# Attention with its scores in one bank and a three-bank tile, divisors formed two units later, and the next image's norm placed beside the projections

## The chip, the cores and the metric

The kernel runs on one core of one Trainium2 chip, as one launch. The metric is device time in microseconds of one execution. A core has five engines with their own instruction queues: TensorE (PE, matmuls; its weight loads are shown as PEld), VectorE (DVE), ScalarE (ACT), GpSimd (POOL) and SyncE (SP, which here only issues DMAs). They are ordered among each other by semaphores alone. PE writes into PSUM, which is eight banks of 2 KB per partition (512 float32 each); ACT and DVE read it.

## The reference

Four images of 256 channels and 48 x 48 pixels go through two layers, each added to its input. All arithmetic is float32.

```python
x = x + L0(_gn(x))      # _gn: group norm, 32 groups
x = x + L1(_gn(x))

def L0(Vx, ...):        # 3x3 conv, batch norm, relu, then attention with 8 heads of 32 channels
    x = relu(bn(conv(Vx, conv_w) + conv_b))          # N = 48*48 = 2304 pixels
    q, k, v = split(einsum('oc,bchw->bohw', qkv_w, x) + qkv_b)
    attn = softmax(einsum('bhdn,bhdm->bhnm', q, k) * 32 ** -0.5, axis=-1)
    out = einsum('bhem,bhnm->bhen', v, attn)
    return einsum('oc,bchw->bohw', proj_w, out) + proj_b

def L1(x, ...):         # guidance conv, 5 branches of 9 shifted taps weighted by a softmax
    guidance = conv3x3(x, W_cat)                     # 45 channels
    outs = [x] + [dyn_branch(x, softmax(guidance[:, 9*i:9*i+9]), d)
                  for i, d in enumerate((1, 6, 12, 24, 36))]
    y = conv1x1(concat(outs), W_scale)
    return batch_norm_over_all_images(y) * gamma + beta
```

## The kernel before, in words

Everything of an image stays in SBUF: channels on the 128 partitions in two halves (`NH = 2`), pixels along the free axis. Two kinds of stages alternate. In an **attention stage** (function `attention`) image b is attended to. In a **mixed stage** (`dynamic_filters`) the second layer of image b is computed by DVE and POOL, and the convolution and the q, k, v of image b + 1 are woven into it for PE. The program is issued in one written order (`tc.manual_schedule()`): each engine executes its instructions in the order of the Python code, and a tile pool makes an instruction wait where a buffer is still in use.

**An attention stage** is cut into nine units. Units 0 to 7 are 512 queries of one half of the heads (four heads, j = 0 to 3, on four groups of 32 partitions); unit 8 holds the last 256 queries of both halves. A unit loops over the keys in 18 steps of 128 (`m`). A step (u, m) is:

- `scores(u, m)`: four matmuls k^T q, one for each head, side by side on 32 rows of the array each, 128 x 512 results. They go to PSUM tiles `se`. Before, these are two tiles of two banks (a pair of heads in each), from a pool of three such tiles (`ps_s`, bufs=3, six banks). Two ACT instructions then form p = exp(scale * s), 128 x 1024 each (L961). `p` has four buffers.
- `weigh(u, m - 1, p)`: one step behind, four matmuls v p, side by side on 32 columns each, add into the PSUM tile `num` (one bank, one buffer, L982). DVE adds p to the running sum `acc` (L999, 128 x 2048) from which the softmax's divisors come. In the steps `LENT = (2, 5, 8, 11, 14)` DVE adds only heads 0 and 1 (128 x 1024); heads 2 and 3 of that p are summed into the SBUF tile `extra` by a DMA that POOL issues (L1001 writes, L1003 accumulates). At the unit's last step DVE adds `extra` to `acc` (L991), and ACT copies `num` to SBUF (L1008) so that the next unit can begin in its one bank.
- `close(u - 1)`, at m = 2 of the next unit: four matmuls of ones with `acc` give the divisors (`den`, a bank of its own, L1014); DVE transposes, inverts and transposes back (L1023 to L1026), and multiplies into the result `ao` (L1031).
- `project(chunk)`, at m = 6 of units 2, 4, 6 (two chunks) and 8: eight matmuls of 384 columns on finished `ao` (L1063), a bias and residual addition and statistics on DVE (L1072, L605), and a DMA to HBM. The sixth chunk is done at the start of the mixed stage.
- The group norm of image b + 1 (b < 3): `finish` (three short stages of statistics with two tiny matmuls in the `den` bank) and twelve ACT instructions that normalize the next image in place (L1715, 128 x 384 each). They are the list `spare`, of which one is taken at each step from m = 3 of unit 2.

The eight PSUM banks of the stage are thus three pairs for scores and projections, `num`, and `den`.

**Around the stage.** At the end of a mixed stage `done(5)` copies the last chunk's y from PSUM to an SBUF tile `y` with ACT (L1301), DVE takes statistics, and SP sends it to HBM (L1309). `load_pad(b)` and `load_pad(b + 1)` then load x into the two padded images (L1692), behind it on SP. The tiles `p` of the attention stage lie in the memory that the mixed stage's tiles leave.

Of the kernel before, what the change touches and what calls it, by code (L numbers as in the profile page):

```python
# [8 lines left out]
F32 = mybir.dt.float32  # L9
F32R = mybir.dt.float32r  # L10
AF = mybir.ActivationFunctionType
# [6 lines left out]
P = 128  # L18
NH = C // P
# [29 lines left out]
def conv_preact_kernel(  # L49
# [482 lines left out]
    with tc.tile_pool(name="w", bufs=1) as wpool, tc.tile_pool(  # L532
# [394 lines left out]
        def attention(b, q, k_, vT, pools, spare, project, scratch):  # L927
# [3 lines left out]
            ao = keep("h", f"ao_{b}")  # L931
            zeros = work0.tile([P, D], F32, tag="zeros", name=f"zeros_{b}", bufs=1)
            nc.gpsimd.memset(zeros, 0.0)
            out = scratch[:, :QC]

            extra = scratch[:, QC : 3 * QC].rearrange("p (j n) -> p j n", j=2)
            scratch = work0.tile([P, QC], F32, tag="rt", name=f"rt_{b}", bufs=1)

            whole, rest = N // QC * QC, N % QC
# [2 lines left out]
            assert NH * rest == QC  # L942
            heads = [slice(j * D, (j + 1) * D) for j in range(4)]

            def ps2(name):
                return ps_s.tile([P, 2, 512], F32, tag="s", name=name)

            def scores(u, m):
                ss = [ps2(f"se_{b}_{u}_{m}_{pair}") for pair in range(2)]
                for g, q0, n, at in units[u]:  # L950
                    for j, r in enumerate(heads):
                        nc.tensor.matmul(  # L952
                            ss[j // 2][:, j % 2, at : at + n],
                            k_[r, g, m * P : (m + 1) * P],
                            q[r, g, q0 : q0 + n],
                            start=True,
                            stop=True,
                        )
                p = work0.tile([P, 4, QC], F32, tag="p", name=f"p_{b}_{u}_{m}", bufs=4)
                for pair in range(2):  # L960
                    nc.scalar.activation(  # L961
                        p[:, 2 * pair : 2 * pair + 2, :], ss[pair], AF.Exp, scale=QS
                    )
                return p

            state = {}

            def weigh(u, m, p):
                if m == 0:
                    state[u] = dict(  # L970
                        num=ps_a.tile([P, 512], F32, tag="num", name=f"num_{b}_{u}"),
                        acc=work0.tile([P, 4, QC], F32, tag="acc", name=f"acc_{b}_{u}"),
                    )
                st = state[u]
                several = len(units[u]) > 1
                if several and m == 0:

                    for j, r in enumerate(heads):
                        nc.tensor.matmul(st["num"][r, :], zeros, p[:, j, :], start=True, stop=False)
                for i, (g, q0, n, at) in enumerate(units[u]):  # L980
                    for j, r in enumerate(heads):
                        nc.tensor.matmul(  # L982
                            st["num"][r, at : at + n],
                            vT[:, m, g * P + j * D : g * P + (j + 1) * D],
                            p[:, j, at : at + n],
                            start=(m == 0 and not several),
                            stop=(m == NT - 1 and i == len(units[u]) - 1),
                        )
                end = u == len(units) - 1
                if m == NT - 1:  # L990
                    nc.vector.tensor_tensor(st["acc"][:, 2:], st["acc"][:, 2:], extra, ALU.add)  # L991
                if end and m == NT - 1:
                    sums(u, p, True, False)
                elif m == 0:
                    st["first"] = p
                else:
                    other = st["first"] if m == 1 else st["acc"]
                    js = slice(0, 2 if m in LENT else 4)
                    nc.vector.tensor_tensor(st["acc"][:, js], other[:, js], p[:, js], ALU.add)  # L999
                    if m == LENT[0]:  # L1000
                        nc.gpsimd.dma_start(out=extra, in_=p[:, 2:])  # L1001
                    elif m in LENT:
                        nc.gpsimd.dma_start(out=extra, in_=p[:, 2:], accum_op=ALU.add)  # L1003
                if end:
                    st["out"] = st["num"]
                elif m == NT - 1:
                    st["out"] = out
                    nc.scalar.copy(out, st["num"])  # L1008

            def sums(u, rhs, start, stop):  # L1010
                if start:
                    state[u]["den"] = ps_a.tile([P, 512], F32, tag="den", name=f"den_{b}_{u}")
                for j, r in enumerate(heads):
                    nc.tensor.matmul(  # L1014
                        state[u]["den"][r, :], ones, rhs[:, j, :], start=start, stop=stop
                    )

            def close(u):

                sums(u, state[u]["acc"], u < len(units) - 1, True)  # L1020
                st = state.pop(u)
                t = scratch
                nc.vector.transpose(t, st["den"])  # L1023
                rc = work0.tile([P, QC // D], F32, tag="rc", name=f"rc_{b}_{u}")
                nc.vector.reciprocal(rc, t.rearrange("p (k d) -> p k d", d=D)[:, :, 0])
                nc.vector.transpose(  # L1026
                    t.rearrange("p (k d) -> p k d", d=D),
                    rc.unsqueeze(2).to_broadcast([P, QC // D, D]),
                )
                for g, q0, n, at in units[u]:  # L1030
                    nc.vector.tensor_tensor(  # L1031
                        ao[:, g, q0 : q0 + n], st["out"][:, at : at + n], t[:, at : at + n],
                        ALU.mult,
                    )

            steps = [(u, m) for u in range(len(units)) for m in range(NT)]
            prev = None
            chunk = 0
            for i, (u, m) in enumerate(steps):
                ps = scores(u, m)  # L1040
                if prev is not None:
                    weigh(*steps[i - 1], prev)
                prev = ps
                if m == 2 and u:
                    close(u - 1)
                if m == 6 and u % NH == 0:
                    while (chunk + 1) * CH <= units[u][0][1]:
                        project(chunk, ao, ps2(f"pp_{b}_{chunk}"))
                        chunk += 1
                if m > 2 and u > 1 and spare:  # L1050
                    spare.pop(0)(ps_a)
            while spare:
                spare.pop(0)(ps_a)
            weigh(*steps[-1], prev)
            close(len(units) - 1)
            return ao, chunk

        def project(b, c, ao, pp, norm):
# [42 lines left out]
        def dynamic_filters(b, ao, chunk, norm, other, pools):  # L1101
# [192 lines left out]
            def done(c):  # L1294
                cols = slice(c * CH, (c + 1) * CH)
                if alone:
                    yc = homes[c]
                else:
                    yc = work1.tile([P, NH, CH], F32, tag="y", name=f"y_{b}_{c}", bufs=1)
                of = py.pop(c)[:, :, :CH]  # L1300
                nc.scalar.copy(yc, of)  # L1301
                free["y"].append(clock("ACT", 800, clock.t["PE"]))
                if c < NCK - 1:
                    of = yc
                    clock("DVE", 1100, free["y"][-1])
                for o in range(NH):
                    nc.vector.bn_stats(yst[:, o, b * NCK + c, :], of[:, o, :])
                if not alone:
                    nc.sync.dma_start(out=y_d[b, :, :, cols], in_=yc)  # L1309

# [256 lines left out]
        for b in range(B + 1):  # L1569
# [130 lines left out]
            if b + 1 < B:  # L1700
                load_pad(b + 1)
                u_next = taken(ORDER[0])
                fin = [None]

                def step(ps_a, nn=nn, fin=fin, b=b):
                    if fin[0] is None:
                        fin[0] = nn.finish(
                            lambda name: ps_a.tile([P, 512], F32, tag="den", name=name)
                        )
                    if next(fin[0], fin) is fin:  # L1710
                        nn.shift_of()

                def piece(h, r0, b=b, nn=nn):
                    t = inside(pads[(b + 1) % 2], h, r0, R)
                    return lambda ps_a: nc.scalar.activation(  # L1715
                        t, t, AF.Identity, bias=nn.shift[:, h : h + 1], scale=nn.rstd[:, h : h + 1]
                    )

                spare = [("den", step)] * 3 + [
                    ("any", piece(h, r0)) for h in range(NH) for r0 in range(0, HH, R)  # L1720
                ]
            norm1 = Norm("n1", b)
            q, k_, vT = qkv[b]
            with tc.tile_pool(name=f"work0_{b}", bufs=2) as work0, tc.tile_pool(
                name=f"ps_s_{b}", bufs=3, space=PSUM
            ) as ps_s, tc.tile_pool(name=f"ps_a_{b}", bufs=1, space=PSUM) as ps_a:
                ao, chunk = attention(
                    b, q, k_, vT, (ps_s, ps_a, work0), [f for _, f in spare],
                    lambda c, ao, pp, b=b, n=norm1: project(b, c, ao, pp, n), scratch,
                )  # L1730

# [74 lines left out]
```

## Time and profile before

| what | us |
|---|---|
| three runs | 2932.91, 2927.28, 2931.93 (median 2931.93) |
| the profiled execution, its own time | 2929.42 |
| its span, first to last instruction | 2927.6 |
| attention of image 0, first exp to last | 144.4 to 521.3 |
| attention of image 1 | 842.2 to 1228.4 |
| attention of image 2 | 1549.4 to 1935.1 |
| attention of image 3 | 2252.2 to 2628.2 |

The four attention stages are thus 1525 us of the 2927.6; the rest is the mixed stages. The page lists busy time of each engine (PE 95%, DVE 83%, ACT 57%, POOL 41% of the span), then groups of instructions with the mean duration of one. A line of the timeline is: start, length, engine, line of the code, operation, tiles, shapes, count, and in brackets the idle time of the engine just before it with what ended it. A line of the windows view is: stretch, its length, then each engine's busy time with its number of instructions, the granted share of PE's clock, the DMA engines' share and GB/s.

### The profile page before, as it was taken

The numbers are of one execution on the slowest core, as the hardware profiler recorded it, in microseconds if no ns is written. First come the engines' busy times: TensorE is split into PE (matmuls) and PEld (weight loads), VectorE is DVE, ScalarE is ACT, GpSimd is POOL, SyncE is SP. The second block draws the span as 40 slices with busy tenths as digits, with TensorE's granted clock in tenths as the row PEclk, the third lists the DMA queues.
The fourth block names the chain that finished last, engine by engine and source line by source line (L and its number), as shares of the span: only waits on it lengthen the run. The fifth ranks groups of instructions, "written<-read, shape, count | busy, mean of one in ns | idle before, by whom it ended". The sixth has DMA issues, their size and how long they took to land. (4 is left out here: it accounts for less than half of the span.)

```text
span 2927.6 us, 43833 instructions
## 1 busy us (share of the span) xinstructions
PE 2773.1 (95%) x16950; PEld 1246.7 (43%) x16950; DVE 2426.1 (83%) x2574; ACT 1675.2 (57%) x2104; POOL 1205.2 (41%) x1024
## 2 busy tenths in 40 slices
PE   7999999999999999999899999999999999998994
PEld 5622223556542222456562222355555222244562
DVE  6388999789868899778986899978886999986886
ACT  3489888322348988712236988852233888871224
POOL 1010010898840010299791100059986010005894
PEclk9999999999999999999999999999999999998997
DMA  4432333132252233323225333322213333335225
GB/s 179 100 69 64 67 76 71 53 87 86 73 127 62 61 78 69 68 65 95 69 68 124 71 69 69 68 63 76 82 50 85 69 75 67 71 67 218 54 74 204
DMA packets 146233, 244.64 MB, mean 84 GB/s; under 512 B 60952, under 2 KB 111968, under 8 KB 144224
## 3 DMA queue, kind: packets, MB, share of 16 engines
q0 software_dynamic: 26720, 99.79, 15.4%
q1 hardware_dynamic: 76960, 87.31, 10.4%
q10 hardware_dynamic: 42336, 54.66, 7.2%
q8 instruction: 135, 2.21, 0.3%
q14 instruction: 82, 0.67, 0.1%
HBM read 115.02 MB, written 32.33 MB: 50 GB/s over the span
## 5 line engine op out<-in xcount | busy, mean ns | idle before, releaser
L961 ACT ACTIVATE p<-se 128x1024 f32<-128x1024 f32 x1296 | 1260.0, 1027 | 239.7 <-PE se L952 171.2
L999 DVE TENSOR_TENSOR acc<-acc,p 128x2048 f32<-128x2048 f32 (+1 forms) x572 | 1118.4, 1955 | 101.2 <-ACT p L961 55.0
L1459 POOL TENSOR_TENSOR cat<-cat,prod 128x752 f32<-128x752 f32 (+9 forms) x661 | 883.1, 1345 | 133.6 <-DVE prod L1442 96.7
L952 PE MATMUL se<-q,k 32*128 32x512 f32 (+1 forms) x5760 | 819.6, 596 | 12.5 <-ACT p L961 6.2
L982 PE MATMUL num<-p,vT 128*32 128x512 f32 (+1 forms) x5760 | 699.0, 565 | 9.0 <-ACT scratch L1008 7.4
L1442 DVE TENSOR_TENSOR prod<-wb,pad 128x384 f32<-128x384 f32 (+8 forms) x687 | 483.4, 738 | 94.4 <-POOL cat L1459 55.9
L952 PEld LDWEIGHTS se<-q,k 32*128 32x128 f32 x5760 | 299.2, 184 | 533.6 <-issue 368.5
L1003 POOL DMA_DIRECT2D scratch<-p x144 | 122.6, 852 | 922.1 <-ACT p L961 872.9
L1281 PE MATMUL py<-cat,wsc 128*128 128x384 f32 x960 | 349.9, 494 | 9.8 <-POOL cat L1459 8.3
L1382 ACT COPY wb<-ws 128x384 f32<-128x384 f32 (+3 forms) x260 | 121.7, 468 | 371.1 <-DVE prod L1442 237.0
L982 PEld LDWEIGHTS num<-p,vT 128*32 128x32 f32 x5760 | 122.3, 108 | 491.2 <-issue 443.0
L1385 PE MATMUL wb<-w,pick 128*128 128x384 f32 (+3 forms) x628 | 299.7, 509 | 24.7 <-DVE prod L1442 15.8
L1281 PEld LDWEIGHTS py<-cat,wsc 128*128 128x128 f32 x960 | 176.3, 192 | 114.8 <-POOL cat L1459 24.8
L1001 POOL DMA_DIRECT2D scratch<-p x36 | 20.1, 558 | 467.8 <-DVE acc L999 339.2
L1385 PEld LDWEIGHTS wb<-w,pick 128*128 128x128 f32 x628 | 116.5, 190 | 140.2 <-DVE prod L1442 63.4
L851 PE MATMUL pc<-cv_q,u 128*128 128x288 f32 x576 | 160.9, 413 | 7.0 <-DVE cv_q L742 6.2
L1133 PE MATMUL pg<-pad,wcat 128*45 128x384 f32 x864 | 158.4, 498 | 1.6 <-DVE pad L592 1.4
L851 PE MATMUL pc<-cv_k,u 128*128 128x288 f32 x576 | 155.0, 407 | 3.3 <-DVE yt L786 1.8
L884 PE MATMUL pq<-hid,wqkv 128*128 128x384 f32 x384 | 135.5, 492 | 11.8 <-DVE yt L786 11.8
L851 PEld LDWEIGHTS pc<-cv_q,u 128*128 128x128 f32 x576 | 108.3, 192 | 37.3 <-DVE cv_q L742 6.3
L1416 DVE TENSOR_TENSOR cat<-wb,pad 128x768 f32<-128x768 f32 x120 | 114.0, 950 | 11.4 <-PE wb L1385 10.8
L851 PEld LDWEIGHTS pc<-cv_k,u 128*128 128x128 f32 x576 | 106.6, 189 | 32.5 <-DVE yt L786 2.5
(221 smaller groups left out, 1976.4 us busy)
## 6 DMA issues: line engine op xcount, KB each, us to landing
scratch<-p POOLq DMA_DIRECT2D x180, 512.0 KB, 4.5
ws<-w_d ACTq DMA_DIRECT2D x256, 192.0 KB, 3.2
pad<-in_x SPq DMA_DIRECT2D x14, 1152.0 KB, 15.6
u<-u_d SPq DMA_DIRECT2D x18, 768.0 KB, 4.7
x_d<-pad SPq DMA_DIRECT2D x48, 192.0 KB, 2.5
xst<-in_x SPq DMA_DIRECT2D x36, 192.0 KB, 2.4
y_d<-y SPq DMA_DIRECT2D x18, 384.0 KB, 3.4
u_d<-u SPq DMA_DIRECT2D x6, 768.0 KB, 3.7
```

The costliest lines, as they stand in the source:

```text
L851: nc.tensor.matmul(m, u[:, h, kx, o * P : (o + 1) * P], halves[g][:, h, i, :, kx : kx + WW], start=(h == 0 and kx == 0), stop=(h == NH - 1 ...
L884: nc.tensor.matmul(pq[:, :CH], wqkv[:, i, s, g * P : (g + 1) * P], hid[:, i, cols], start=(i == 0), stop=(i == NH - 1),)
L952: nc.tensor.matmul(ss[j // 2][:, j % 2, at : at + n], k_[r, g, m * P : (m + 1) * P], q[r, g, q0 : q0 + n], start=True, stop=True,)
L961: nc.scalar.activation(p[:, 2 * pair : 2 * pair + 2, :], ss[pair], AF.Exp, scale=QS)
L982: nc.tensor.matmul(st["num"][r, at : at + n], vT[:, m, g * P + j * D : g * P + (j + 1) * D], p[:, j, at : at + n], start=(m == 0 and not s ...
L999: nc.vector.tensor_tensor(st["acc"][:, js], other[:, js], p[:, js], ALU.add)
L1003: nc.gpsimd.dma_start(out=extra, in_=p[:, 2:], accum_op=ALU.add)
L1133: nc.tensor.matmul(pg[64 * s : 64 * s + NG, :CH], wcat[:, ii, k, :], window(gn, ii, cc * R, k // 3 - 1, k % 3 - 1), start=(i == 0 and k == 0),
L1281: nc.tensor.matmul(to, wsc[:, n * NH + i, o * P : (o + 1) * P], rhs(i), start=(n == 0 and i == 0), stop=(last and i == NH - 1),)
L1385: nc.tensor.matmul(pw[:, : nr * WW], pick[:, k : k + 1].to_broadcast([P, P]), w[:, l0 * WW : l1 * WW], start=True, stop=True,)
L1442: nc.vector.tensor_tensor(pv, wb, src, ALU.mult)
L1459: nc.gpsimd.tensor_tensor(dst, dst, pv, ALU.add)
```

## The change

1. `scores` writes head 0 to a one-bank tile (`so`, one buffer, pool `ps_a`) and heads 1 to 3 to a three-bank tile (`se`, two buffers, pool `ps_s`). The two exps become 128 x 512 and 128 x 1536.
2. `close` runs two units later: `close(u - 2)` at m = 1 of unit u, ahead of `weigh(u, 0)`; unit 8 also has `close(7)` at m = 2, and the last `close` is at the end as before. `den`, and the projections' results, now take a three-bank tile of the scores' rotation. `num` is copied straight to `ao`, where DVE later multiplies in place.
3. Projections run at m = 6 of units 3, 5, 7 (two chunks) and 8. The next image's norm runs only there: one element of `spare` per chunk, just ahead of the chunk's matmuls; the first (DVE only) at m = 2 of unit 1, two more with the statistics, then three with four of the normalizing instructions each.
4. Unit 0 lends no sums to DMA (DVE adds all four heads in all its steps), and unit 8 lends four times instead of five; its `extra` is added two steps earlier, at m = 15. In the others `extra` is added after the last p, not before it.
5. At the end of the mixed stages of images 0 to 2 the last chunk's y is copied by two ACT instructions into rows of the padded image `gn`, no longer needed, and sent from there with two DMAs.

```diff
             def scores(u, m):
-                ss = [ps2(f"se_{b}_{u}_{m}_{pair}") for pair in range(2)]
+                s1, s3 = ps_a.tile([P, 512], F32, tag="one", ...), three(f"se_{b}_{u}_{m}")
                 for g, q0, n, at in units[u]:
                     for j, r in enumerate(heads):
+                        dst = s3[:, j - 1] if j else s1
                         nc.tensor.matmul(
-                            ss[j // 2][:, j % 2, at : at + n],
+                            dst[:, at : at + n],
...
-                for pair in range(2):
-                    nc.scalar.activation(
-                        p[:, 2 * pair : 2 * pair + 2, :], ss[pair], AF.Exp, scale=QS
-                    )
+                nc.scalar.activation(p[:, 0, :], s1, AF.Exp, scale=QS)
+                nc.scalar.activation(p[:, 1:, :], s3, AF.Exp, scale=QS)
...
-                if m == NT - 1:
-                    nc.vector.tensor_tensor(st["acc"][:, 2:], st["acc"][:, 2:], extra, ALU.add)
...
-                    js = slice(0, 2 if m in LENT else 4)
+                    lend = u > 0 and m in LENT[: len(LENT) - end]
+                    js = slice(0, 2 if lend else 4)
                     nc.vector.tensor_tensor(st["acc"][:, js], other[:, js], p[:, js], ALU.add)
...
-                    nc.scalar.copy(out, st["num"])
+                if u and m == (NT - 3 if end else NT - 1):
+                    rest = st["acc"][:, 2:]
+                    nc.vector.tensor_tensor(rest, rest, extra, ALU.add)
+                if m == NT - 1 and not end:
+                    g, q0, n, _ = units[u][0]
+                    nc.scalar.copy(ao[:, g, q0 : q0 + n], st["num"])
...
-                    state[u]["den"] = ps_a.tile([P, 512], F32, tag="den", ...)
+                    state[u]["den"] = three(f"den_{b}_{u}")[:, 0, :]
...
                 ps = scores(u, m)
+                if m == 1 and u > 1:
+                    close(u - 2)
                 if prev is not None:
                     weigh(*steps[i - 1], prev)
                 prev = ps
-                if m == 2 and u:
+                if m == 2 and u == last:
                     close(u - 1)
-                if m == 6 and u % NH == 0:
-                    while (chunk + 1) * CH <= units[u][0][1]:
-                        project(chunk, ao, ps2(f"pp_{b}_{chunk}"))
+                if m == 6 and (u % NH == 1 or u == last):
+                    while (chunk + 1) * CH <= units[u if u == last else u - 1][0][1]:
+                        pp = three(f"pp_{b}_{chunk}")
+                        if spare:
+                            spare.pop(0)(pp[:, 2, :])
+                        project(chunk, ao, pp)
                         chunk += 1
-                if m > 2 and u > 1 and spare:
-                    spare.pop(0)(ps_a)
-            while spare:
-                spare.pop(0)(ps_a)
+                if m == 2 and u == 1 and spare:
+                    spare.pop(0)(None)
...
+                if c == NCK - 1 and not alone:
+                    rows = gn[:, :, 1 : 1 + R, 1 : 1 + WW]
+                    for o in range(NH):
+                        nc.scalar.copy(rows[:, o], rows_of(of[:, o]))
+                else:
+                    nc.scalar.copy(yc, of)
...
+                    for o in range(NH):
+                        nc.sync.dma_start(out=rows_of(y_d[b, :, o, cols]), in_=rows[:, o])
...
-                spare = [("den", step)] * 3 + [
-                    ("any", piece(h, r0)) for h in range(NH) for r0 in range(0, HH, R)
+                spare = [stats] * 3 + [
+                    lambda t, some=todo[i::3], f=pieces: f(t, some) for i in range(3)
                 ]
...
-                name=f"ps_s_{b}", bufs=3, space=PSUM
+                name=f"ps_s_{b}", bufs=2, space=PSUM
```

## The prediction

> **What bounds the kernel now.** I read the windows view first, one line per unit of image 1 (lengths are from first exp to first exp), then the timeline of an ordinary unit on all engines, then the same for DVE alone.
>
> ```profile
> 842.23:890.12 47.89, 44.93 (x278) 10.70 (x276) 31.11 (x16) 34.80 (x37) 4.13 (x6) 0.86 0.80 168
> 930.10:976.34 46.24, 45.97 (x316) 14.39 (x318) 40.45 (x33) 44.45 (x55) 3.95 (x5) 1.00 0.31 66
> 1016.72:1059.47 42.75, 42.48 (x304) 11.74 (x303) 38.88 (x27) 35.30 (x37) 3.97 (x5) 1.00 0.33 71
> 1059.47:1099.45 39.98, 39.72 (x298) 10.30 (x296) 37.33 (x23) 35.30 (x37) 3.95 (x5) 1.00 0.31 67
> ```
>
> Units 0, 2, 4 and 5: an ordinary unit (5) takes 39.98 us, one with a projected chunk (4) 42.75, unit 2 (a chunk and the norm) 46.24, and unit 0 47.89, at a granted clock of 0.86 and a DMA share of 0.80. In images 0, 2 and 3 the windows give unit 0 38.90, 47.72 and 41.38. PE is "busy" for all of it, but that hides waits inside overlapping matmuls, so I look at starts.
>
> ```profile
> 899.82 1.07 PE L982 MATMUL num<-p,vT 128*32 128x512 f32 x8
> 900.81 1.14 PE L952 MATMUL se<-q,k 32*128 32x512 f32 x8
> 901.89 1.06 PE L982 MATMUL num<-p,vT 128*32 128x512 f32 x8
> 902.05 4.00 ACT L961 ACTIVATE p<-se 128x1024 f32<-128x1024 f32 x4 [0.36 <-PE se L952]
> 902.88 1.37 PE L952 MATMUL se<-q,k 32*128 32x512 f32 x8
> 904.18 1.06 PE L982 MATMUL num<-p,vT 128*32 128x512 f32 x8
> ```
>
> From scores to num is 1.07 to 1.08 us (900.81 to 901.89) and from num to scores 0.99 to 1.00: PE could do a step in 2.07. Every second step the scores last 1.3 instead of 1.14: the second pair's matmuls find its buffer still being read by the exp (that of three steps of the rotation before). Over m = 3 to 17 of unit 5 the exps start 2.16 apart on average. ACT's two exps fit in 1.94, so neither ACT nor PE is full; the three-buffer rotation holds them.
>
> ```profile
> 1066.00 0.72 DVE L1023 STREAM_TRANSPOSE rt<-den 128x512 f32<-128x512 f32 x1
> 1068.40 7.34 DVE L999 TENSOR_TENSOR acc<-acc,p 128x1024 f32<-128x1024 f32 x4
> 1076.19 18.28 DVE L999 TENSOR_TENSOR acc<-acc,p 128x2048 f32<-128x2048 f32 x9 [0.46 <-DVE acc L999]
> 1094.99 4.69 DVE L999 TENSOR_TENSOR acc<-acc,p 128x2048 f32<-128x2048 f32 x2 [0.52 <-ACT p L961]
> ```
>
> DVE is almost full too: unit 5 leaves it idle for about 0.9 us beyond the 0.1 between dependent adds. A full add comes every 2.40 (2.29 + 0.10), a half one every 1.33, `close` takes 2.40 (1066.00 to 1068.40). A unit costs DVE 38.9.
>
> ```profile
> 871.44 1.13 PE L952 MATMUL se<-q,k 32*128 32x512 f32 x4
> 874.10 3.77 ACT L961 ACTIVATE p<-se 128x1024 f32<-128x1024 f32 x4 [3.85 <-DMA scratch<-p]
> 875.17 1.56 PE L952 MATMUL se<-q,k 32*128 32x512 f32 x4 [2.61 <-ACT p L961]
> 876.66 1.94 PE L982 MATMUL num<-p,vT 128*32 128x512 f32 x8
> ```
>
> Unit 0 of image 1: while the images' loads fill the DMA engines, a lent sum holds its p, ACT waits 3.85, PE pauses 2.61, and afterwards eight num matmuls last 1.94 instead of 1.06.
>
> **The change part by part** (sums against the profiled execution, 2929.42; the median of the three runs is 2931.93, 2.5 higher, and the forecast is for that).
>
> *Scores in 1 + 3 banks.* A 128 x 512 evacuation by ACT takes 0.593 (L1008), 128 x 1024 1.023, so 0.84 ns an element and 1.453 for 1536; consecutive exps overlap by 0.10, so a step's pair again fits in 1.94. The scores of m + 1 need the small exp of m, which ends 1.24 + 0.59 = 1.83 after the scores of m began, before 2.07: no wait. The large tiles alternate and are free. What remains is a loop over two steps: scores to exp 1.24, exps 1.94, to num about 0.06, num to scores 1.00: 4.24, or 2.12 a step, just over PE's 2.07. I take 2.11 (head 0's matmul starts a little ahead). Against 2.16 that is 0.05 a step.
>
> *Closes two units later, den in the rotation.* Before, the first three steps of a unit took 2.29 + 2.35 + 2.92 = 7.56. After, counted from scores(u, 0): scores(u, 1) at 2.07; den at 3.23, when the large exp of step 0 has freed the buffer; num, queued on PE behind den, at 4.23, which covers its wait for the copy of `num` (over at 3.73); scores(u, 2) must wait for the large exp of step 1, which the copy pushed to end at 5.50, so 5.56; scores(u, 3) at 7.63. That needs DVE's transpose of den: the last add of u - 1, `extra` (1.33) and the transpose end at 5.45 plus DVE's lag, so it waits only if DVE is more than 2.1 behind. Unit: 7.63 + 15 x 2.11 = 39.3 against 39.98, and 38.9 is DVE's floor. Units 2 to 7 gain 0.68 each, 4.1 an image. Unit 1 closes nothing (no den: 6.8 + 31.65 = 38.45), gain 1.5. Unit 8 closes two: 0.68 less 1.2 = -0.5. Together 5.1 x 4 = 20.4.
>
> *Norm beside projections.* Unit 2 loses its 46.24 - 42.76 = 3.5 in images 0 to 2: 10.4. The cover: a chunk's matmuls hold the scores back 2.7 to 2.8 (42.75 - 39.98; 45.33 for two), so ACT has 2.9 free; four instructions of 0.76 with the usual overlap take 2.7, eight beside two chunks 5.4 of 5.6. The chunk with the root has two table loads (1.28 each) and DVE's inverse, 2.8. If the cover were missing, 12 x 0.66 = 8 an image would come back. DVE, with 2.4 a chunk, must free pp's tile before the second scores after it, due 2.07 after the chunk and ready at 1.9.
>
> *No lent sums in unit 0.* DVE does 17 full adds, 40.7 from the second p on, against 18 x 2.11 = 38.0 of PE, and falls 4.6 behind; the small exp of step m + 4 is due 4 x 2.11 - 1.94 = 6.5 after p(m), and DVE's add takes 2.4, so the four p buffers allow 4.1 and 0.5 is lost, and unit 1 (36.5 of DVE) takes it back to 2.1. Unit 0 becomes 38.5, in image 0 0.4 less. Image 3 starts cold (2.5 over image 0) and keeps that: 0.4. Images 1 and 2 also lose their stall: 47.89 - 41.0 and 47.72 - 41.0, 13.6. Here a rule is weighed. PE's clock, by the rows:
>
> ```profile
> 870.00:874.00 4.00, 2.56 (x20) 0.46 (x12) 1.89 (x2) 0.25 (x1) 0.00 (x0) 1.00 0.96 283
> 874.00:883.00 9.00, 7.83 (x32) 1.58 (x36) 5.81 (x3) 5.71 (x6) 0.97 (x2) 0.62 0.32 67
> ```
>
> A pause of 2.61 was followed by a clock of 0.62 over nine us. The Trainium skill, "TensorE: Matmul & The Clock Gate", section "HAM oscillation", warns only of pauses over about 3.4 us. By the rule the pause would have cost only itself and removing it about 3.4 an image less (half of the 6.8 us at half clock): 6.8 less in total. I take the row. POOL issues six transfers fewer an image (0.85 each); nothing queues behind it in this stage, so that is worth nothing. The same page, "A second HAM failure mode", speaks against the change: short PE idles between groups while cycling PSUM can make the clock oscillate. Units 2 to 8 idle 0.2 us in every second step at 1.00, so I charge nothing, but the new waits (0.3 at scores(u, 2)) are of that kind.
>
> *Tail.* `extra`'s addition (1.22) leaves the end of unit 8. The sums over acc could then start 0.5 earlier, when those over p are done: 2.0 in all.
>
> *Last y.* ACT's first exp waits for the y transfer (3.14 idle at 842.23, scores done at about 841.6): 0.5 x 3 = 1.5. Two copies for one cost 0.1. Two transfers of rows (2.5 us to land like x_d's) stand ahead of the loads on SP, and the second image's load also waits for their landing; that is about 2.5 us later for data first normalized 300 us later. Bounds 0 and 1 either way. The new copies overwrite rows that the last taps have read already.
>
> Sum: 20.4 + 10.4 + 14.4 (unit 0) + 2.0 + 1.5 = 48.7, so 2929.4 - 48.7 = 2880.7, and 2883 on the median.
>
> **The rivals.**
>
> *DVE binds and the shared rotation couples it to PE* (20%). DVE has 38.9 of 39.3; if it stays over 2.1 behind, scores(u, 3) wait for den and projections for pp's tile, and units stay near 40. For: 0.1 between dependent adds is pure loss, unit 0 leaves it 4 behind. Against: chunks give DVE 0.35 each to catch up. Then the 20.4 goes, and some tail: 28 gained, 2904.
>
> *PE is not held by the loop* (15%): steps of 2.07, units on DVE's floor, 38.9. 0.4 x 28 = 11 more: 2872.
>
> *The lent sums' stall moves on* (5%): unit 1's first transfers meet the loads. The loads landed by about 870, unit 1 begins near 883. 2897.
>
> *Slower: the three-bank exp is dearer* (4%). The trace has no exp over 1024. Every 0.1 us on it lengthens the two-step loop by 0.1, and 648 steps by 32. At 0.15 (1.60 instead of 1.45) the gain is gone; at 1.70 the kernel takes 2964. Against it: three points (512, 768 at 0.80, 1024) on one line. A gain is excluded, since elements cost 0.84 ns wherever seen.
>
> **How the numbers follow.** The main case has 56%. Its own range is 2874 to 2893 (unit 38.9 to 39.5, norm cover 0 to 3 lost). The others reach from 2868 to 2908, and the range takes those of 2872 and 2904 in: 2866 to 2906. A difference under 0.2% (5.9 us) can't be told from none by runs that spread over 5.6. Slower 0.04, same 0.03, faster 0.93.
>
> **What would show it.** Right: steps of 2.1 without alternation; exps of 0.59 and 1.45; units 0 of images 1 and 2 near 41 at a clock over 0.9; no unit with ACT over 36 outside the chunks' units; den's matmuls ahead of the unit's first num. Wrong: scores waiting for DVE's transpose at m = 3; a 1536 exp above 1.5; pieces of the norm delaying exps after a chunk; unit 1 with waits for DMA; a granted clock below 1.00 in units 2 to 8.

## The result, and the profile after

The changed kernel takes 2888.39 us, the median of four runs (2880.53 to 2890.83), against 2932.42 of the kernel before on the same chip: 0.9848 of its time, with a 95% interval of 0.9825 to 0.9871. That is 44.0 us less; the forecast was 2883.0, or 48.9 less. The profiled execution took 2887.44, with a span of 2885.7 (before 2927.6, so 41.9 less).

The totals of the page say little: PE was busy for 2773.1 us before and is for 2726.2 now, DVE for 2426.1 and 2445.6. Of its groups, the two exps (the last numbers are the sum in us, the mean in ns, and the idle time before):

```profile
L963 ACT ACTIVATE p<-se 128x1536 f32<-128x1536 f32 x648 | 938.4, 1448 | 0.0
L962 ACT ACTIVATE p<-so 128x512 f32<-128x512 f32 x648 | 388.5, 600 | 183.8 <-PE se L954 81.5
```

They answer one open question at once: an exp over three banks takes 1.448 us where the forecast had 1.453, and one over 512 takes 0.600 where it had 0.593. The rival in which the three-bank exp is dearer is gone.

The windows view of image 1 (length, then busy us of PE, PEld, DVE, ACT and POOL, the granted clock, DMA share and GB/s) shows units 0, 3, 4, 5 and 6:

```profile
836.72:875.12 38.40, 37.75 (x284) 8.69 (x288) 32.10 (x14) 34.91 (x36) 0.00 (x0) 0.96 0.73 146
952.50:995.24 42.74, 41.99 (x310) 10.90 (x314) 39.19 (x27) 35.73 (x40) 3.97 (x5) 1.00 0.33 72
995.24:1034.08 38.84, 38.84 (x300) 9.16 (x304) 37.04 (x23) 35.19 (x37) 3.95 (x5) 1.00 0.31 68
1034.08:1080.19 46.11, 43.93 (x312) 11.89 (x316) 39.68 (x30) 37.97 (x40) 4.00 (x5) 0.96 0.31 66
1080.19:1118.97 38.78, 38.78 (x300) 9.17 (x304) 36.98 (x23) 35.23 (x37) 3.97 (x5) 1.00 0.32 69
```

An ordinary unit (4 and 6) takes 38.8 where it took 39.98; unit 0 takes 38.40 where it took 47.89, at a clock of 0.96 for 0.86. Against that stand unit 3, and above all unit 5: 46.11 at 0.96, as much as unit 2 took before with its chunk and the norm (46.24). A chunk and the last of the norm's statistics are together there now.

From first exp to last, the four attention stages take 368.4, 369.9, 369.4 and 365.5 us (before 376.9, 386.2, 385.7, 376.1): 51.7 less. The time outside them has grown by 9.8.

The timeline of an ordinary step of image 1, and then of DVE in unit 6 (here and below, only the rows that bear on the reading are shown):

```profile
976.53 1.06 PE L983 MATMUL num<-p,vT 128*32 128x512 f32 x8
976.62 0.60 ACT L962 ACTIVATE p<-so 128x512 f32<-128x512 f32 x1
977.12 1.45 ACT L963 ACTIVATE p<-se 128x1536 f32<-128x1536 f32 x1
977.53 0.69 PE L954 MATMUL so<-q,k 32*128 32x512 f32 x1
978.60 1.07 PE L983 MATMUL num<-p,vT 128*32 128x512 f32 x8
978.69 0.60 ACT L962 ACTIVATE p<-so 128x512 f32<-128x512 f32 x1
```

```profile
1087.62 2.29 DVE L999 TENSOR_TENSOR acc<-p,p 128x2048 f32<-128x2048 f32 x1
1090.02 32.90 DVE L999 TENSOR_TENSOR acc<-acc,p 128x1024 f32<-128x1024 f32 x16
```

A step is 2.07 (976.62 to 978.69), every step alike: 1.00 from num to scores (976.53 to 977.53) and 1.07 from scores to num (to 978.60), which is what PE alone was taken to need. The scores begin at 977.53 and their exp at 978.69, 1.16 later; the forecast had taken 1.24 for this. On DVE the sixteen adds of the unit follow one another without a mark of idle time, but they hardly hold PE back: every step from m = 6 on is 2.07, and the three before it take 6.40 together.

### The profile page after: what moved, and what is told of

Read it like the earlier page. It is cut to its first block, busy times and chain, and to the rows that moved or that the text cites. A ratio compares the mean times of both kernels' runs of the same rounds, so it can differ in the third digit from the quotient of the medians.

```text
span 2885.7 us, 43628 instructions
## 1 busy us (share of the span) xinstructions
PE 2726.2 (94%) x16950; PEld 1202.4 (42%) x16950; DVE 2445.6 (85%) x2570; ACT 1677.0 (58%) x2107; POOL 1190.2 (41%) x1000
## 5 line engine op out<-in xcount | busy, mean ns | idle before, releaser
L999 DVE TENSOR_TENSOR acc<-acc,p 128x2048 f32<-128x2048 f32 (+1 forms) x572 | 1144.2, 2000 | 59.9 <-ACT p L963 3.2
L963 ACT ACTIVATE p<-se 128x1536 f32<-128x1536 f32 x648 | 938.4, 1448 | 0.0
L954 PE MATMUL se<-q,k 32*128 32x512 f32 (+1 forms) x4320 | 738.9, 594 | 0.1
L954 PE MATMUL so<-q,k 32*128 32x512 f32 (+1 forms) x1440 | 730.6, 595 | 8.9 <-DVE bound L922 6.0
L962 ACT ACTIVATE p<-so 128x512 f32<-128x512 f32 x648 | 388.5, 600 | 183.8 <-PE se L954 81.5
L954 PEld LDWEIGHTS so<-q,k 32*128 32x128 f32 x1440 | 216.6, 183 | 524.9 <-ACT p L962 478.4
L1003 POOL DMA_DIRECT2D scratch<-p x124 | 105.6, 852 | 770.6 <-ACT p L963 732.1
L983 PEld LDWEIGHTS num<-p,vT 128*32 128x32 f32 x5760 | 131.4, 108 | 480.0 <-issue 446.8
L1001 POOL DMA_DIRECT2D scratch<-p x32 | 17.9, 559 | 572.4 <-ACT p L963 521.7
L954 PEld LDWEIGHTS se<-q,k 32*128 32x128 f32 x4320 | 227.5, 183 | 5.5 <-ACT p L963 4.1
```

The lines of the kernel that those rows point to most:

```text
L954: nc.tensor.matmul(dst[:, at : at + n], k_[r, g, m * P : (m + 1) * P], q[r, g, q0 : q0 + n], start=True, stop=True,)
L962: nc.scalar.activation(p[:, 0, :], s1, AF.Exp, scale=QS)
L963: nc.scalar.activation(p[:, 1:, :], s3, AF.Exp, scale=QS)
L983: nc.tensor.matmul(st["num"][r, at : at + n], vT[:, m, g * P + j * D : g * P + (j + 1) * D], p[:, j, at : at + n], start=(m == 0 and not s ...
```

## The experiments

All edits are to the changed kernel unless another is named. Ratios are to the kernel before, run on the same chip in the same turn; the changed kernel itself stands at 0.9848.

**The bank layout alone undone.** Scores go back to two two-bank tiles from three buffers, the divisors and projections take that rotation too, and the statistics get a bank of their own. Closes, norm, lent sums and tail stay as changed.

```diff
-                s1, s3 = ps_a.tile([P, 512], F32, tag="one", ...), three(f"se_{b}_{u}_{m}")
+                ss = [three(f"se_{b}_{u}_{m}_{pair}") for pair in range(2)]    # three: now two banks, bufs=3
...
+                for pair in range(2):
+                    nc.scalar.activation(p[:, 2 * pair : 2 * pair + 2, :], ss[pair], AF.Exp, scale=QS)
...
-                            spare.pop(0)(pp[:, 2, :])
+                            spare.pop(0)(ps_a.tile([P, 512], F32, tag="one", ...))
```

> The changed kernel with scores in three rotating two-bank tiles again (exps 128 x 1024 twice); den and the projections take a tile of that rotation, the norm's statistics get the freed bank. Theory A (the bank layout set the step): steps alternate 2.07 and 2.25 again, about 2.16 on average, and an ordinary unit goes from 38.8 to about 40.0; 28 units make it some 30 us slower than the changed kernel, while units 3 and 5 lose their excess from the statistics (1.1 and 4.4 us, images 0 to 2), since these no longer share a projection's tile, for 16 us back. Theory B (the later divisors alone freed PE): steps stay at 2.07, ordinary units at 38.8.

Measured: 2914.91 (2 runs), ratio 0.9944 (0.9924 to 0.9964), some 26 us more than the changed kernel, where 14 were expected (30 lost, 16 back). A step in its timeline, image 1:

```profile
977.12 1.37 PE L954 MATMUL se<-q,k 32*128 32x512 f32 x8
978.42 1.07 PE L985 MATMUL num<-p,vT 128*32 128x512 f32 x8
```

The scores of 1.3 before the next num are back (977.12 to 978.42), short steps (2.02 to 2.12) alternate with long ones (2.19 to 2.30), and an ordinary unit is 39.95, the 39.98 of before. So the steps' gain is the layout's. One more thing is to be seen: unit 5, with the statistics in a bank of their own, is 44.5 here, 4.6 over an ordinary unit; in the changed kernel, where they share the chunk's tile, it is 7.3 over. Of the 16.3 us by which units 3 and 5 of images 0 to 2 exceed those of image 3 in the changed kernel, 9.5 come back, not 16. The layout alone is therefore worth more than 26: an estimate from the two numbers is 36.

**The divisors one unit later, as before.** The layout stays; `close(u - 1)` at m = 2.

```diff
-                if m == 1 and u > 1:
-                    close(u - 2)
...
-                if m == 2 and u == last:
+                if m == 2 and u:
                     close(u - 1)
```

> The changed kernel with close(u - 1) at m = 2 of unit u in all units, one unit earlier. Theory A (DVE is now a co-limit, its last add of a unit starts 1.75 us after its p): den's matmuls wait for acc and the extra addition, which end about 1.75 + 2.3 + 1.3 = 5.4 us after the unit's last p, while PE reaches them about 5.3 after it; so PE waits little, 0 to 1 us a unit, but loses the cover of num's wait for its copy (1 us a unit): ordinary units 39.5 to 40.5, 25 to 45 us slower in all. Theory B (it does not matter when the divisors are formed): units stay at 38.8 within 0.2 us, below 6 us in all.

Measured: 2881.95 (2 runs), ratio 0.9831 (0.9812 to 0.9851). The loss of 25 to 45 us did not come. The windows of units 1, 2 and 8 of image 1:

```profile
870.86:911.29 40.43, 38.22 (x300) 8.60 (x296) 38.65 (x25) 35.36 (x37) 3.99 (x5) 1.00 0.30 66
911.29:950.19 38.90, 38.48 (x300) 8.87 (x304) 37.20 (x23) 35.29 (x37) 3.97 (x5) 1.00 0.32 69
...
1158.38:1200.97 42.59, 41.54 (x578) 22.15 (x578) 39.26 (x26) 37.68 (x41) 3.12 (x4) 1.00 0.28 61
```

An ordinary unit is 38.9, as with the later close. Unit 1, which closes again, is 2.1 longer than the 38.36 of the changed kernel, unit 8, which closes once at m = 2, 0.6 to 0.9 shorter. Unit 5 is 43.3 to 43.7 instead of 45.7 to 46.1, at a full clock: its pause fell otherwise. In image 3, which has no norm, units 1 to 8 take 327.6 here and 326.3 in the changed kernel, so forming the divisors later pays about 1 us an image. That the whole kernel is 6 us faster without it is no evidence on the closes: unit 5 gives 7 of it, and the two intervals overlap.

**Unit 0 lends sums again.**

```diff
-                    lend = u > 0 and m in LENT[: len(LENT) - end]
+                    lend = m in LENT[: len(LENT) - end]
...
-                if u and m == (NT - 3 if end else NT - 1):
+                if m == (NT - 3 if end else NT - 1):
```

> The changed kernel with unit 0 lending its sums to DMA again. Theory A (the lent transfers meet the loads): unit 0 of images 1 and 2 goes from 38.4 to 44 to 48 us with an ACT wait for a DMA near step 11 and a PE clock below 0.9; image 0's is within 1 us of 37.3; 12 to 20 us slower in all. Theory B (the loads were harmless and the stall came from the old y transfer or from the pair buffers): below 4 us.

Measured: 2897.92 (2 runs), ratio 0.9886 (0.9866 to 0.9906), 9.5 more than the changed kernel where 12 to 20 were expected; in the profiled execution the attention stages are 12.5 longer. Unit 0 of images 1 and 0 (windows view), and the stall in image 1's (timeline):

```profile
833.85:880.57 46.72, 41.21 (x284) 9.31 (x288) 30.91 (x16) 34.80 (x37) 4.03 (x5) 0.89 0.84 176
144.18:181.43 37.25, 36.94 (x287) 8.56 (x288) 30.89 (x16) 34.79 (x36) 3.99 (x5) 1.00 0.33 72
```

```profile
866.82 0.60 ACT L962 ACTIVATE p<-so 128x512 f32<-128x512 f32 x1 [4.28 <-DMA scratch<-p]
867.47 0.72 PE L954 MATMUL so<-q,k 32*128 32x512 f32 x1 [3.58 <-ACT p L962]
```

Where the DMA share is 0.84, ACT waits 4.28 for a lent p and the clock falls to 0.89 (image 2 is alike, at 47.46). In image 3, at a share of 0.62, that wait is 1.51; in image 0, at 0.33, the same unit takes 37.25, the 37.33 of the changed kernel. It is the meeting with the loads that costs, not the lending. About 1.5 us of the difference in images 1 and 2 is not the lending's: these units begin with 6.8 us at half clock here and 3.4 in the changed kernel, and that varies without an edit (see the last section).

**The statistics behind the chunk's matmuls.** The changed kernel forms them in the third bank of `pp` just ahead of the chunk; here they come just behind it.

```diff
-                        if spare:
-                            spare.pop(0)(pp[:, 2, :])
-                        project(chunk, ao, pp)
+                        project(chunk, ao, pp, spare.pop(0) if spare else None)
...  in project, after the eight matmuls:
+            if beside:
+                beside(pp[:, 2, :])
```

> The changed kernel with the norm's statistics matmuls issued behind a chunk's eight matmuls, not ahead of them. Theory A (the chunk's matmuls wait, in the same tile, for ACT's and DVE's reads of the statistics): unit 3 falls from 42.75 to about 41.6 and unit 5 from 46 to about 42.5 (about 1 us stays for the root and its two table loads ahead of the next exp), 12 to 15 us faster than the changed kernel in all, and the half-clock window in unit 5 is gone. Theory B (the table loads on ACT are what holds unit 5): unit 5 stays above 45.

Measured: 2876.04 (2872.74 to 2878.72, 4 runs), ratio 0.9807 (0.9791 to 0.9824), 12 less than the changed kernel. The timeline of unit 5 in image 1, first of the changed kernel, then of this one:

```profile
1049.02 0.38 PE L627 MATMUL pp<-mvn,gmat 128*128 128x2 f32 x2
...
1050.45 1.23 DVE L999 TENSOR_TENSOR acc<-acc,p 128x1024 f32<-128x1024 f32 x1 [0.46 <-ACT p L963]
1051.60 0.15 DVE L87 TENSOR_SCALAR grstd_n<-pp 128x2 f32<-128x2 f32 x1
1051.81 4.54 PE L1069 MATMUL pp<-ao,wp 128*128 128x384 f32 x8 [2.18 <-DVE grstd_n L87]
1057.43 0.60 ACT L962 ACTIVATE p<-so 128x512 f32<-128x512 f32 x1 [4.15 <-PE se L954]
```

```profile
1045.46 2.85 PE L1067 MATMUL pp<-ao,wp 128*128 128x384 f32 x8
1048.14 0.28 PE L627 MATMUL pp<-mvn,gmat 128*128 128x2 f32 x2
...
1048.88 0.20 ACT L88 ACTIVATE grstd_n<-grstd_n 128x2 f32<-128x2 f32 x1 [1.09 <-DVE grstd_n L87]
1049.10 1.28 ACT L962 ACT_TABLE_LOAD   x1
1050.39 0.60 ACT L962 ACTIVATE p<-so 128x512 f32<-128x512 f32 x1
```

In the changed kernel PE waits 2.18 us with its chunk until DVE has read the statistics of the same tile, although they lie in another bank; and DVE reads them late, behind an add. PE then does most of the chunk at half its clock (4.54 for 2.85; the windows view gives 0.50 from 1052.00 to 1055.41), and ACT sits idle for 4.15. Behind the chunk that wait is gone and the matmuls take 2.85. Unit 5 is 42.4 to 42.6, at a clock of 1.00, and unit 3 41.8 to 42.0, 13 us less over three images; unit 0 of images 1 and 2, in which no line was edited, is 1.5 longer each, at a lower clock (0.93 granted from 833 to 880).

**And unit 8's `extra` by PE.** On top of that, unit 8 lends five times again, DVE adds no `extra` there, and two matmuls of ones add it into the divisors.

```diff
-                    lend = u > 0 and m in LENT[: len(LENT) - end]
+                    lend = u > 0 and m in LENT
...
-                if u and m == (NT - 3 if end else NT - 1):
+                if u and m == NT - 1 and not end:
...  in close:
+                if u == last:
+                    sums(u, extra, False, False, 2)
```

> The kernel with the statistics behind the chunk's matmuls, and in unit 8 five lent sums again, whose transferred part PE adds to the divisors with two matmuls of ones instead of DVE's addition at m = 15. Theory A (DVE's lag sets the end of the stage: its last add starts 3.6 us after its p): DVE has 2.4 us less in unit 8, the lag falls to about 1.2, the time from the last exp to DVE's transpose of den from 5.0 to about 3, and the half-clock window after it from 6.8 to 3.4 in most images; 8 to 14 us faster than with the statistics moved alone, about 2865. Theory B (the stage's end is hidden by the mixed stage's work): the tail shortens and the time moves under 4 us.

Measured: 2870.25 (2866.75 to 2875.11, 5 runs), ratio 0.9787 (0.9774 to 0.9801), 6 us less than with the statistics moved alone, where 8 to 14 were expected; the two intervals overlap. The end of image 0's stage (timeline), first in the kernel before, then in the changed kernel, then here:

```profile
519.38 1.94 ACT L961 ACTIVATE p<-se 128x1024 f32<-128x1024 f32 x2 [0.30 <-PE se L952]
521.92 1.23 DVE L991 TENSOR_TENSOR acc<-acc,scratch 128x1024 f32<-128x1024 f32 x1
524.30 0.72 DVE L1023 STREAM_TRANSPOSE rt<-den 128x512 f32<-128x512 f32 x1 [1.16 <-PE den L1014]
```

```profile
512.24 1.45 ACT L963 ACTIVATE p<-se 128x1536 f32<-128x1536 f32 x1
513.91 1.22 DVE L1006 TENSOR_TENSOR acc<-acc,scratch 128x1024 f32<-128x1024 f32 x1
515.24 2.29 DVE L999 TENSOR_TENSOR acc<-acc,p 128x2048 f32<-128x2048 f32 x1
517.59 1.07 PE L1015 MATMUL den<-acc,ones 128*32 128x512 f32 x8 [1.93 <-DVE acc L999]
518.72 0.72 DVE L1024 STREAM_TRANSPOSE rt<-den 128x512 f32<-128x512 f32 x1 [1.19 <-PE den L1015]
521.41 5.26 PE L1069 MATMUL pp<-ao,wp 128*128 128x384 f32 x8 [2.75 <-DVE ao L1034]
```

```profile
509.50 1.44 ACT L963 ACTIVATE p<-se 128x1536 f32<-128x1536 f32 x1
512.75 0.60 PE L1015 MATMUL den<-scratch,ones 128*32 128x512 f32 x2
513.61 1.03 PE L1015 MATMUL den<-acc,ones 128*32 128x512 f32 x4
514.68 0.72 DVE L1026 STREAM_TRANSPOSE rt<-den 128x512 f32<-128x512 f32 x1 [2.22 <-PE den L1015]
517.37 4.42 PE L1069 MATMUL pp<-ao,wp 128*128 128x384 f32 x8 [2.73 <-DVE ao L1036]
```

From the end of the last exp to DVE's transpose it was 2.98 before (521.32 to 524.30) and 5.03 in the changed kernel (513.69 to 518.72), and is 3.74 here (510.94 to 514.68). In the changed kernel the addition of `extra`, though written two steps before the end, starts only after the last exp has ended, as DVE is that far behind, and the last add starts 3.6 behind its p. Here that lag is 1.3, about the 1.2 that was expected. The tail, expected at about 3, stayed 0.75 above that of before. The half clock after the stages, expected at 3.4 us in most images instead of 6.8, lasts 3.4, 0, 6.8 and 6.8 us in images 0 to 3.

**And the second half of the statistics in the divisors' tile.** On top of both, the second pair of statistics matmuls goes into a free bank of the divisors' tile at `close(3)`, in unit 5, so that only the root and the inverse stay beside that chunk.

```diff
-                rstd_of(rstd, pv[:, :NH])
+                nc.vector.tensor_scalar(rstd, pv[:, :NH], EPS, None, ALU.add)
+                yield
+                nc.scalar.activation(rstd, rstd, AF.Sqrt)
+                nc.vector.reciprocal(rstd, rstd)
...  in close:
+                if u == 3 and spare:
+                    spare.pop(0)(st["more"])
...
-                spare = [stats] * 3 + [
+                spare = [stats] * 4 + [
```

> As the one before, and the second pair of statistics matmuls moved into the divisors' tile of unit 3 (formed in unit 5 at m = 1), with only the root, its tables and DVE's inverse left beside the second chunk. Theory A (what is left in unit 5 is the root's chain behind the chunk): unit 5 falls from 42.6 to about 41.8, 2 to 3 us faster in all. Theory B (the tables themselves delay the next exp): unit 5 stays at 42.6.

Measured: 2866.89 (2858.68 to 2870.55, 5 runs), ratio 0.9778 (0.9760 to 0.9796), the best of all; its lead over the one before it, 3.4 us where 2 to 3 were expected, is less than either spreads. The trace shows the step itself. Timeline, unit 5 of image 1:

```profile
1040.73 2.85 PE L1075 MATMUL pp<-ao,wp 128*128 128x384 f32 x8
...
1043.07 0.20 ACT L631 ACTIVATE grstd_n<-grstd_n 128x2 f32<-128x2 f32 x1
1043.29 1.28 ACT L965 ACT_TABLE_LOAD   x1
1044.66 0.60 ACT L965 ACTIVATE p<-so 128x512 f32<-128x512 f32 x1
```

The root and the first of its two table loads now lie beside the chunk's matmuls, the second load ends while the next scores run (1044.57), and the exp starts with the scores' own 1.15 (from 1043.51). Unit 5 is 42.1 in image 0 and 41.7 in images 1 and 2; that of image 3, which has no norm, is 41.98.

**The last y as before**, copied to a tile of its own and sent from there.

```diff
-                if c == NCK - 1 and not alone:
-                    rows = gn[:, :, 1 : 1 + R, 1 : 1 + WW]
...
+                    nc.scalar.copy(yc, of)
...
-                    for o in range(NH):
-                        nc.sync.dma_start(out=rows_of(y_d[b, :, o, cols]), in_=rows[:, o])
+                nc.sync.dma_start(out=y_d[b, :, :, cols], in_=yc)
```

> The changed kernel with the last chunk's y copied to its own tile and sent from there, as before. Theory A (the first exp waits for that transfer): from the first scores to the first exp 1.8 to 1.9 us instead of 1.2 in images 1 to 3, 2 us slower in all if the clock's windows fall alike. Theory B (the two smaller copies and transfers cost as much as they save): no difference at the entry.

Measured: 2888.58 (2 runs), ratio 0.9853 (0.9835 to 0.9871). At the entry to image 1's attention it shows in the timeline: the first exp waits for y's transfer and starts 2.08 after its scores did (835.53), where the changed kernel needs 1.19.

```profile
837.61 0.60 ACT L962 ACTIVATE p<-so 128x512 f32<-128x512 f32 x1 [3.29 <-DMA y_d<-y]
```

The same wait stands in images 2 and 3; over images 1 to 3 the entries are 2.0 us longer (0.9, 0.9 and 0.25). The total, 0.2 above that of the changed kernel, shows nothing of it.

## Why the prediction came out so

The time came within its range and 5 us above its value, but of its five terms two were too small and two had the wrong sign. That these errors nearly cancel is luck. By the profiled executions (forecast 48.7 less, measured 41.9):

| term | forecast | measured | from |
|---|---|---|---|
| steps and closes | 20.4 | 34 | units 2 to 7 of image 3, which has no norm: 251.0 to 244.2, so 6.8 an image; unit 1 1.6; unit 8 about 0.2 |
| norm beside projections | 10.4 | -5.9 | 3.5 an image gone from unit 2, 10.4; units 3 and 5 of images 0 to 2 longer than image 3's by 1.1 and 4.1 to 4.5 |
| unit 0 | 14.4 | 22.5 | 1.6, 9.5, 9.3 and 2.1 in images 0 to 3 |
| tail | 2.0 | -7.7 | last exp to transpose, after less before, four images |
| last y | 1.5 | 1.6 | entries: 0.7, 0.7 and 0.2 less |

They add to 44.5, 2.6 more than was measured. Outside them, the first stage starts 0.9 later (145.32 for 144.41), and the first chunk after a stage takes 0.6 to 1.0 longer in each image (5.26 for 4.51 in image 0); the rest, under 2, was not followed up.

*Steps and closes.* The mechanism was right, as the layout undone shows. The mis-sized term is the 1.24 from scores to exp. It was read at one step of the kernel before (900.81 to 902.05); two steps later there the same way took 1.17 (timeline):

```profile
905.18 1.14 PE L952 MATMUL se<-q,k 32*128 32x512 f32 x8
906.35 3.09 ACT L961 ACTIVATE p<-se 128x1024 f32<-128x1024 f32 x3 [0.31 <-PE se L952]
```

In the new layout it is 1.16 in almost every step, so the loop over two steps is 1.16 + 1.94 + 0.06 + 1.00 = 4.16, within the reading the same as two of PE's own 2.07. The rival "PE is not held by the loop" had this. Which part of the layout makes the steps alike, head 0's own bank or the two buffers of the large tile, was not tried apart. The first three steps of a unit, forecast at 7.63, measured 7.54 from exp to exp. In units 2 to 7 the working gave the later close nothing (7.63 for 7.56), and an ordinary unit is indeed 38.8 or 38.9 with either close. What the later close gives to unit 1, unit 8 takes back in part.

*DVE binding PE.* With 38.9 us of work, by the forecast's count, in a unit of 38.8, DVE stays 1.1 to 3.6 behind its p through the ordinary units without falling further back, and no scores wait for it there to speak of. One exp a unit does: in unit 6 that of m = 4 starts at 1090.01, 1.37 after its scores, as DVE still holds the p buffer, which costs the unit about 0.2. So that rival came only in small part, but its cause appeared at the stage's end.

*The norm.* The step that failed is "The cover". It asked only whether ACT had time beside a chunk, and DVE behind it. For the twelve normalizing instructions that was right: unit 7 takes 44.21 in images 0 to 2 as in image 3. For the statistics it overlooked that their matmuls and the chunk's write one tile, and that the chunk therefore waits until ACT and DVE have read it, DVE behind an add. The sign flipped in two places of an image, and a sign that the prediction itself had named for being wrong came with it, a granted clock below 1.00 in units 2 to 8 (0.96 in unit 5). Statistics behind the chunk bring back 12 us of the 16, which settles it.

*Unit 0.* The mechanism was right: lending again brings the stall back. The mis-sized term is the 41.0 for a unit that starts cold: it is 38.4 in images 1 and 2. Part of that is the faster step, and that the 0.5 forecast for DVE's lag is not lost, although the lag reaches 5.0: image 0's unit 0, at full clock, takes 37.33, where 38.5 was forecast. The rest is luck: the unit begins with one stretch of 3.4 us at half clock, where the forecast's 2.5 over image 0 came from two; with the statistics moved, the same code has two and takes 39.9. What the rows said of the pause, that removing 2.61 us of idle PE also removes the slow time after it, held; the Trainium skill's limit of about 3.4 us ("TensorE: Matmul & The Clock Gate", "HAM oscillation") would have missed it, and missed again the 2.18 us in unit 5, after which the chunk ran at half clock. Its second rule, of short idles ("A second HAM failure mode"), was not seen: ordinary units stay at 1.00, in the old layout too, where PE idles 0.2 us in every second step.

*Tail.* The step that failed is "leaves the end of unit 8". DVE works in order and had no spare time in the last steps, so an addition moved ahead by two steps gains nothing: the add behind it starts later by its length. In unit 8 DVE has also a full add for a half one, since it lends one less. The lag of its last add is 0.5 before, 3.6 in the changed kernel and 1.3 with one more lent and the addition left to PE, which brought 1.3 an image in the tail; the two edits were made together, so their shares stay open. The second close in unit 8 is not the cause: with `close(u - 1)` as before, where unit 8 has one close less, lag and tail are 3.6 and 5.03 again in images 0 to 2. The faster steps have a part: with the layout undone and the rest of unit 8 as changed, they are 2.9 and 4.08.

*Last y.* Right in size at the entries, and too small to show in the runs.

## What to carry to other kernels

Give each pipelined result a rotation deep enough that the loop between two engines is no longer than the steps of the engine that should bind. Here that was worth over 26 us, and the moment at which a unit is closed about 1 us an image. Before you put a small task beside a large one, ask which tile it writes and who must read that before the large one may go on: put it behind, or in another tile. And on an engine without spare time count every instruction to the end of the stage; an addition is removed by not doing it there, not by doing it earlier.

## What the runs showed of the hardware that was not expected

Pauses of PE of about two us were followed by half clock: 2.18 us in unit 5 by 3.4 us (a granted clock of 0.50 from 1052.00 to 1055.41; the eight matmuls took 4.54 for 2.85), and 1.93 at the stage's end, with 2.75 close behind it, by 6.8 us (0.50 from 519.52 to 526.34; 5.26 for the chunk). In the kernel before, the stage's end has one pause of 2.73 and 3.4 us at 0.50 (527.59 to 531.00; 4.51).

Such a pause does not settle it alone. At the start of image 1's attention the code is the same in three of the kernels, and PE pauses for 1.99 and 0.70 us in each. Half clock follows for 3.4 us in the changed kernel, not at all with the earlier closes, and for 6.8 us with the statistics moved; unit 0 takes 38.4, 37.4 and 39.9. What decides between them was not found. A difference of a us or two in a stage that starts cold is thus no evidence on an edit elsewhere. Nor did taking pauses away raise the mean clock each time: in the profiled executions it was 0.979 in the changed kernel, 0.979 with the statistics moved, though unit 5 is then at 1.00, and 0.983 in the last version.
